# Row maxima of a quartered softmax: through memory instead of a masked product

## The chip, the cores and the metric

The kernel runs on one core of a Trainium2 chip. A core has a matrix engine (TensorE, PE in the profile), a vector engine (VectorE, DVE), an activation engine (ScalarE, ACT), a general engine (GpSimd, POOL) and an engine that only issues transfers (SyncE, SP). Each works through its own queue of instructions in order; semaphores tie the queues together. PE writes to PSUM[...]; all else lies in SBUF, on 128 partitions; DRAM is reached by DMA. The metric is the time of one execution on the device in microseconds.

## The reference, cut to what matters

The whole is one layer: a cross attention with residual, a block that sends a quarter of the tokens through self attention and the rest through a state-space scan, and a mixture of experts. The change lies in the cross attention:

```
sim = einsum("bihd,bjhd->bhij", q1, k) * scale   # 4 batches, 8 heads, 256 queries, 4096 + 256 keys
attn = softmax(sim, axis=-1)                     # subtracts each query's maximum over all keys
out = einsum("bhij,bjhd->bihd", attn, v)
```

All is in 32-bit floats. The softmax must hold for every query over its 4352 keys.

## The kernel before

The attention walks over 16 groups `G`, one for each batch and pair of heads, and in each over 8 blocks of 32 queries: 128 steps, numbered `n`, with `s` the number within the group. The keys of a group are cut into four quarters of 1088. In `scores(n)` (L1279, L1287) quarter `q` of the scores of the 32 queries goes to partitions 32q to 32q+31 of `su`, five PSUM banks that there are once only, so that a query has four partitions, one for each quarter, and both heads of the pair lie side by side. `su` is thus 128 partitions by 2 times 1088.

`copy_max(n)` (L1299) copies both halves out of `su` on DVE and keeps the maximum of each partition in `nm`, 128 by 2. These are maxima of quarters. To get a query's maximum, the kernel before does three things:

- on DVE it multiplies `nm`, repeated four times, by `quarter`, a mask that leaves the maxima of quarter q in columns of q alone: `mq`, 128 by 4 by 2 (L1306);
- in `stat(n)` PE multiplies `mq` by `same` (L1311), which has a 1 wherever two partitions belong to one query. Each partition then holds the four maxima of its query in eight columns (four quarters, two heads), in a free corner of `su`;
- DVE reduces them to `nb`, the negated maximum (L1316).

`exps(n)` (L1327, ACT) takes the exponential with `nb` as bias and sums it. `turn(n, j)` (L1336, DVE) transposes blocks of 32 by 32, and `values` (L1345, PE) multiplies four steps' worth by the values; this happens in steps with `s % 4 == 1`. `k_chunk` (L1226) and `v_chunk` (L1263) make keys and values of the same or the next group, three chunks in most other steps; ACT copies each from one of three PSUM banks (L1214, L1267). Their input `ctx` is loaded by SP through four buffers (L1130).

The order of instructions is written out by hand in one loop over `n`. One step issues: `scores(n)`, `exps(n-1)`, `copy_max(n)`, the first piece (a chunk, or nine key blocks of the values product), some background work, the second piece, then `turn(n-1, 0)`, `stat(n)`, `turn(n-1, 1)`, the third piece and background work again. In the steps with values `stat(n)` follows the second piece and both transposes come at the end. `slot(budget)` is what inserts background work: the router, the token attention, the scan and the expert ordering of the batches that are finished, whose generators yield a time until they are due and an amount of DVE time. The clock `now` that it compares with is advanced by hand-set estimates, 0.3 for `stat`. The scan (L632 to L652) runs on ACT (`da`), POOL (`db`, `y`) and DVE (L644) together.

After the attention, at about 1260 us, the scan of the last batch and the experts follow.

Of the kernel before, what the change touches and what calls it, by code (L numbers as in the profile page):

```python
# [8 lines left out]
F32 = mybir.dt.float32  # L9
AF = mybir.ActivationFunctionType  # L10
ALU = mybir.AluOpType
AX = mybir.AxisListType
PSUM = bass.MemoryType.PSUM

P = 128
# [22 lines left out]
def bc(ap, axis, n):  # L38

    ap = ap.unsqueeze(axis)  # L40
    shape = list(ap.shape)
    shape[axis] = n
    return ap.to_broadcast(shape)
# [3 lines left out]
def perceiver_layer(ctx: ExitStack, tc: tile.TileContext, a: dict, out: bass.AP):  # L47
    nc = tc.nc
# [5 lines left out]
    dram = ctx.enter_context(tc.tile_pool(name="dram", bufs=2, space=bass.MemoryType.DRAM))  # L54
    fin = ctx.enter_context(tc.tile_pool(name="fin", bufs=1))
# [999 lines left out]
    now = [0.0]  # L1055
    active = []

    def start(g):
        active.append([g, now[0], 0.0])
# [36 lines left out]
    SU = (0, 2 * 512 + 512 - (QK - SQ))  # L1096
    SC = (0, 3 * 512)
    SX = (2 * 512, SU[1])
    SM = 2 * 512 + 128
    NHP = H // 2  # L1100
    NG = B * NHP
    NJ = QK // 32
    with ExitStack() as s1:
        ctp = s1.enter_context(tc.tile_pool(name="xctx", bufs=4))
        wk = s1.enter_context(tc.tile_pool(name="xwk", bufs=2))
# [12 lines left out]
        def load_qk(G):  # L1118
            return load_weights(G, ("wk2",), "wk2", 2)

        def load_self(G):
            return load_weights(G, ("wk1", "wq1"), "wself", 1)
# [26 lines left out]
        def load_later():  # L1149
# [7 lines left out]
            yield from load_consts()  # L1157
            start(routed(0))

        same = fin.tile([P, 4, 32], F32, name="same")  # L1160
        dm = same[:, 0, :]
        nc.vector.tensor_reduce(
            out=dm, in_=ident.rearrange("p (c i) -> p i c", c=4), axis=AX.X, op=ALU.add
        )
        for q in range(1, 4):
            nc.vector.tensor_copy(same[:, q, :], dm)
        quarter = fin.tile([P, 4, 2], F32, name="quarter")
        nc.vector.tensor_reduce(
            out=quarter[:, :, 0], in_=ident.rearrange("p (c i) -> p c i", c=4), axis=AX.X,
            op=ALU.add,  # L1170
# [27 lines left out]
        su = ps_s.tile([P, 5 * 512], F32, name="su")  # L1198
# [7 lines left out]
        for t in qzs:  # L1206
            nc.gpsimd.memset(t, 0.0)
        kts, qTs, vts, sps, nbs, pts, pos, aos, lss = ({} for _ in range(9))
        mqs, nms = {}, {}

        def keys_out(G, k0, ps):

# [80 lines left out]
        def copy_max(n):  # L1293
            nms[n] = wk.tile([P, 2], F32, tag="nm", name="nm")
            sps[n] = [
                wk.tile([P, QK], F32, tag=f"sp{j}", name=f"sp{j}") for j in range(2)
            ]
            for j in range(2):
                nc.vector.tensor_scalar(  # L1299
                    out=sps[n][j], in0=su[:, SU[j] : SU[j] + QK], scalar1=1.0, scalar2=None,  # L1300
                    op0=ALU.mult, op1=ALU.max, accum_out=nms[n][:, j : j + 1],
                )


            mq = mqs[n] = wk.tile([P, 4, 2], F32, tag="mq", name="mq")
            nc.vector.tensor_tensor(mq, bc(nms[n], 1, 4), quarter, ALU.mult)  # L1306

        def stat(n):

            st = su[:, SM : SM + 8]  # L1310
            nc.tensor.matmul(  # L1311
                st, same.rearrange("p q i -> p (q i)"),
                mqs[n].rearrange("p q j -> p (q j)"), start=True, stop=True,
            )
            nbs[n] = wk.tile([P, 2], F32, tag="nb", name="nb")
            nc.vector.tensor_reduce(  # L1316
                out=nbs[n], in_=st.rearrange("p (q j) -> p j q", q=4), axis=AX.X, op=ALU.max,
                negate=True,
            )

        def exps(n):
            G, s = divmod(n, 8)
            b, hp = divmod(G, NHP)
            if n % 32 == 0:
                lss[b] = fin.tile([P, NHP, 8, 2], F32, tag="ls", name="ls", bufs=2)
            for j in range(2):
                nc.scalar.activation(  # L1327
                    sps[n][j], sps[n][j], AF.Exp, bias=nbs[n][:, j : j + 1],
                    accum_out=lss[b][:, hp, s, j : j + 1],
                )  # L1330
# [86 lines left out]
        with tc.manual_schedule():  # L1417
            norms = {}
            k_chunk(0, 0)
            wself[0] = load_self(0)  # L1420
            nc.scalar.dma_start(out=bo_bc, in_=a["xbo"].partition_broadcast(P))
            for _ in norm(0):
                pass
            for g in range(1, NCH):
                k_chunk(0, g)
                if g == 4:
                    turn_x(0)
            k_self(0)
            start(load_later())
            wv[0] = load_v(0)  # L1430
            N = 8 * NG
            for n in range(N + 2):
                G, s = divmod(n, 8)
                new, old = n < N, 1 <= n <= N


                pieces, took = [], 1.75
                if s == 5 and G + 1 < NG:
                    wv[G + 1] = load_v(G + 1)
                if s % 4 == 1:  # L1440
                    m, took = n // 4 - 1, 1.95
                    if m >= 0:
                        pieces = [
                            lambda i=i: values(m, i, min(i + 9, NJ)) for i in range(0, NJ, 9)
                        ]
                elif 2 <= s <= 4 and G < NG:
                    pieces = [
                        lambda g=g: v_chunk(G, g) for g in range(3 * s - 6, 3 * s - 3)
                    ]
                elif G + 1 < NG:  # L1450
                    if s == 0:
                        wqk[G + 1] = load_qk(G + 1)
                        wself[G + 1] = load_self(G + 1)
                    pieces = {
                        0: [lambda g=g: k_chunk(G + 1, g) for g in range(3)],
                        6: [lambda g=g: k_chunk(G + 1, g) for g in range(3, 6)],
                        7: [lambda: k_self(G + 1)]
                        + [lambda g=g: k_chunk(G + 1, g) for g in range(6, 8)],
                    }[s]


                tail = n >= N - 2

                def piece(i):
                    if i < len(pieces):
                        pieces[i]()
                    if i < len(pieces) or tail:
                        now[0] += took

                if new:  # L1470
                    scores(n)
                    now[0] += 2.1
                if old:
                    exps(n - 1)
                if new:
                    copy_max(n)
                piece(0)
                if s % 4 != 1:
                    slot(1.3)
                    piece(1)  # L1480
                    if old:
                        turn(n - 1, 0)
                    if new:
                        stat(n)
                        now[0] += 0.3
                    if s == 0 and n:
                        sums(G - 1)
                        now[0] += 0.2
                    if old:
                        turn(n - 1, 1)  # L1490
                    slot(1.3 if tail else 0.5)
                    piece(2)
                    slot(2.9)
                else:
                    last = s == 1 and G
                    if last:
                        spread(G - 1)
                        now[0] += 0.6
                    slot(1.5)
                    piece(1)  # L1500
                    if new:
                        stat(n)
                        now[0] += 0.3
                    slot(2.8)
                    if last:
                        normalize(m - 1)
                    if n == N + 1:

                        psx[B - 1] = bank("psx")
                        project(B - 1, 0, psx[B - 1], range(NHP))  # L1510
                        add(B - 1, 0, psx[B - 1])
                        project(B - 1, 1, psx[B - 1], range(NHP - 1))
                    piece(2)
                    slot(1.5)
                    piece(3)
                    if n > 4:
                        values_out(m)
                    if old:
                        turn(n - 1, 0)
                        turn(n - 1, 1)  # L1520
                    if last:
                        normalize(m)
                        if m % 8 == 7:
                            start_first(finish_batch(m // 8))
                b = n // 32 + 1
                if b < B:
                    if n % 32 == 20:
                        norms[b] = norm(b)
                    if n % 32 in (20, 22):
                        next(norms[b])  # L1530
                    if n % 32 == 29:
                        turn_x(b)
# [299 lines left out]
```

## Time and profile before

| what | value |
|---|---|
| median of three runs | 1555.44 us (1549.75 to 1558.04) |
| the profiled execution | 1555.58 us, of which the span of instructions is 1553.9 |
| PE, DVE, ACT, POOL busy in the span | 94%, 68%, 49%, 27% |
| mean granted PE clock | 0.977 of full speed |
| L1299, copy with maximum, DVE, 256 times | 1281 ns each |
| L1306, multiply to `mq`, DVE, 128 times | 167 ns median |
| L1311, the product, PE, 256 passes | 256 ns median |
| L1316, reduce to `nb`, DVE, 128 times | 128 ns median |
| L1327, exponential, ACT, 256 times | 1195 ns each |

A row of the group table or the timeline reads: line of the kernel, engine, operation, output and inputs by their names in the program, shapes, number of instructions, then busy time and mean, and in brackets how long the engine had been idle and what it had waited for. A 32-bit product is two passes on PE, so the trace counts 256 for 128 products. "PEld" is the loading of weights, which can lie beside matmuls. Matmuls are pipelined: their durations overlap, and what one costs is read from the distance of the pieces around it. The chain of work that ended last follows the program back from its last instruction, at each step to what released it; a piece in it is time on the path.

### The profile page before, as it was taken

The numbers are of one execution on the slowest core, as the hardware profiler recorded it, in microseconds if no ns is written. First come the engines' busy times: TensorE is split into PE (matmuls) and PEld (weight loads), VectorE is DVE, ScalarE is ACT, GpSimd is POOL, SyncE is SP. The second block draws the span as 40 slices with busy tenths as digits, with TensorE's granted clock in tenths as the row PEclk, the third lists the DMA queues.
The fourth block names the chain that finished last, engine by engine and source line by source line (L and its number), as shares of the span: only waits on it lengthen the run. The fifth ranks groups of instructions, "written<-read, shape, count | busy, mean of one in ns | idle before, by whom it ended". The sixth has DMA issues, their size and how long they took to land.

```text
span 1553.9 us, 37283 instructions
## 1 busy us (share of the span) xinstructions
PE 1461.9 (94%) x15686; PEld 1039.5 (67%) x15686; DVE 1057.1 (68%) x1812; ACT 758.9 (49%) x1486; POOL 412.0 (27%) x464
## 2 busy tenths in 40 slices
PE   7999999999999999999999999999998868988799
PEld 3757667576667475766665767757665558778587
DVE  1666666666699976565999866658988633499453
ACT  3444454454666644555667454546664413534211
POOL 1000000000089940000799500005996011110100
PEclk9999999999999999999999999999999968999899
DMA  7445543524344525243454343334543115777471
GB/s 240 149 131 160 161 139 107 180 72 143 120 147 140 182 83 192 79 145 100 141 176 158 113 144 126 99 112 162 159 127 114 42 55 183 253 250 259 125 233 48
DMA packets 157767, 223.41 MB, mean 144 GB/s; under 512 B 14976, under 2 KB 76160, under 8 KB 157600
## 3 DMA queue, kind: packets, MB, share of 16 engines
q1 hardware_dynamic: 152368, 211.45, 42.7%
q10 hardware_dynamic: 3744, 5.51, 1.1%
q0 software_dynamic: 1488, 4.07, 0.9%
q8 instruction: 124, 2.03, 0.5%
q14 instruction: 43, 0.35, 0.1%
HBM read 216.56 MB, written 4.42 MB: 142 GB/s over the span
## 4 chain that ended last, share of the span: by engine, by line
PE 63%; POOL 14%; DVE 13%; issue 4%; ACT 3%; DMA 2%; ACTq 0%; SPq 0%; DVEq 0%; POOLq 0%
PE po L1345 12%; PE su L1279 11%; PE psv L1263 11%; PE psk L1226 9%; POOL y L652 5%; POOL db L637 5%; POOL db L650 4%; DVE sp L1299 4%; PE su L1287 2%; PE pg L1749 2%; PE pu L1749 2%; PE pde L1762 2%; DVE pt L1336 2%; DVE db L739 1%; DVE db L644 1%
## 5 line engine op out<-in xcount | busy, mean ns | idle before, releaser
L1299 DVE TENSOR_SCALAR_CACHE_REDUCE sp<-su 128x1088 f32<-128x1088 f32 x256 | 318.8, 1281 | 182.0 <-PE su L1287 182.0
L1336 DVE STREAM_TRANSPOSE pt<-sp 128x1088 f32<-128x1088 f32 x256 | 328.0, 1295 | 57.0 <-PE po L1345 56.9
L1327 ACT ACTIVATE sp<-sp,nb 128x1088 f32<-128x1088 f32 x256 | 305.2, 1195 | 13.9 <-DVE nb L1316 13.7
L1345 PE MATMUL po<-pt,v 128*64 128x128 f32 x4352 | 263.9, 278 | 2.3 <-DVE pt L1336 1.3
L1279 PE MATMUL su<-kt,qz 64*32 64x512 f32 x4096 | 256.0, 609 | 4.4 <-DVE nb L1316 3.7
L1226 PE MATMUL psk<-ctx,wk 128*128 128x512 f32 x512 | 245.1, 612 | 10.2 <-DMA ctx<-in_ctxT 7.7
L1345 PEld LDWEIGHTS po<-pt,v 128*64 128x64 f32 x4352 | 241.7, 139 | 14.1 <-issue 7.7
L1263 PE MATMUL psv<-wv,ctx 128*128 128x128 f32 x2048 | 250.3, 279 | 0.6 <-DMA ctx<-in_ctxT 0.3
L1263 PEld LDWEIGHTS psv<-wv,ctx 128*128 128x128 f32 x2048 | 236.1, 192 | 6.7 <-issue 1.4
L1226 PEld LDWEIGHTS psk<-ctx,wk 128*128 128x128 f32 x512 | 91.4, 191 | 94.3 <-issue 85.0
L1214 ACT COPY kt<-psk 128x512 f32<-128x512 f32 x128 | 74.8, 585 | 158.6 <-PE psk L1226 158.4
L1279 PEld LDWEIGHTS su<-kt,qz 64*32 64x32 f32 x4096 | 63.3, 108 | 124.4 <-issue 93.0
L652 POOL TENSOR_TENSOR y<-y,db 128x192 f32<-128x192 f32 x192 | 135.2, 704 | 15.1
L1267 ACT COPY v<-psv 128x512 f32<-128x512 f32 x144 | 79.2, 558 | 119.8 <-PE psv L1263 118.5
L644 DVE TENSOR_TENSOR_SCAN db<-da,db 128x384 f32<-128x384 f32 x96 | 123.2, 1284 | 14.4 <-POOL db L637 3.7
L650 POOL TENSOR_TENSOR db<-db,cb 128x384 f32<-128x384 f32 x96 | 110.8, 1154 | 26.4 <-DVE da L642 26.4
L395 POOL TENSOR_TENSOR kbd<-qk,hmask 128x512 f32<-128x512 f32 x8 | 8.2, 1045 | 407.1 <-ACT qk L385 407.1
L637 POOL TENSOR_TENSOR db<-bb,xc 128x384 f32<-128x384 f32 x96 | 111.2, 1181 | 0.2
L1287 PEld LDWEIGHTS su<-kt,qz 128*32 128x32 f32 x2048 | 34.6, 109 | 109.3 <-issue 109.3
L632 ACT ACTIVATE da<-delta,A_log_sb 128x192 f32<-128x192 f32 x192 | 75.4, 447 | 51.1 <-DVE da L642 38.4
L1382 ACT COPY ao<-po 128x128 f32<-128x128 f32 x32 | 8.5, 264 | 152.5 <-PE po L1345 152.5
L1311 PEld LDWEIGHTS su<-mq,same 128*128 128x128 f32 x256 | 41.1, 191 | 54.7 <-DVE mq L1306 37.8
(278 smaller groups left out, 1587.2 us busy)
## 6 DMA issues: line engine op xcount, KB each, us to landing
ctx<-in_ctxT SPq DMA_DIRECT2D x256, 512.0 KB, 4.8
gateT<-in_gateT SPq DMA_DIRECT2D x27, 512.0 KB, 4.0
upT<-in_upT SPq DMA_DIRECT2D x27, 512.0 KB, 5.1
downT<-in_downT SPq DMA_DIRECT2D x27, 512.0 KB, 6.2
bb<-bcd SPq DMA_DIRECT2D x24, 192.0 KB, 4.3
cb<-bcd SPq DMA_DIRECT2D x24, 192.0 KB, 3.6
wv<-in_wv SPq DMA_DIRECT2D x32, 128.0 KB, 2.4
in_w<-in_in_w SPq DMA_DIRECT2D x32, 128.0 KB, 3.8
```

The lines of the kernel that those rows point to most:

```text
L637: nc.gpsimd.tensor_tensor(db, bbs[k], bc(xc[:, m, :], 1, SG), ALU.mult)
L644: nc.vector.tensor_tensor_scan(out=db, data0=da, data1=db, initial=0.0, op0=ALU.mult, op1=ALU.add,)
L650: nc.gpsimd.tensor_tensor(db, db, cbs[k], ALU.mult)
L652: nc.gpsimd.tensor_tensor(y[:, m, :], y[:, m, :], db[:, s, :], ALU.add)
L1226: nc.tensor.matmul(ps, wqk[G][:, 0, c, :], ct[:, c, :], start=(c == 0), stop=(c == KD - 1),)
L1263: nc.tensor.matmul(ps[:, i * P : (i + 1) * P], lhsT, wv[G][:, w, c, :], start=(c == 0), stop=(c == KD - 1),)
L1267: nc.scalar.copy(v.rearrange("p k d -> p (k d)"), ps[:, : n * P])
L1279: nc.tensor.matmul(su[q * 32 : (q + 1) * 32, SC[j] + lo : SC[j] + lo + 512], qT[r, j, s * 32 : (s + 1) * 32], kt[r, q, lo : lo + 512], sta ...
L1299: nc.vector.tensor_scalar(out=sps[n][j], in0=su[:, SU[j] : SU[j] + QK], scalar1=1.0, scalar2=None, op0=ALU.mult, op1=ALU.max, accum_out=nm ...
L1327: nc.scalar.activation(sps[n][j], sps[n][j], AF.Exp, bias=nbs[n][:, j : j + 1], accum_out=lss[b][:, hp, s, j : j + 1],)
L1336: nc.vector.transpose(pts[m, j][:, i, :], sps[n][j])
L1345: nc.tensor.matmul(pos[m][j * HD : (j + 1) * HD, :], vts[m // 2, k // 4][:, k % 4, j * HD : (j + 1) * HD], pts[m, j][:, :, kk * 32 : (kk + ...
```

## The change

The mask, the multiply and the product go. Instead, the maxima of the quarters are written to a small tensor in DRAM, `md`, in which a query's four quarters lie next to each other, and are read back with a source that repeats for the four groups of partitions. Each partition then has its query's eight values in SBUF, and the same reduce makes `nb` of them. Both transfers are issued from ACT's queue. `send_max(n)` comes after the first piece, `fetch_max(n)` where `stat(n)` was, and `stat(n-1)`, now only the reduce, comes in the next step between `scores(n)` and `exps(n-1)`. Of `same` only its first quarter, `dm`, is left, which other parts use.

```diff
-        same = fin.tile([P, 4, 32], F32, name="same")
-        dm = same[:, 0, :]
+        dm = fin.tile([P, 32], F32, name="dm")
...
-        for q in range(1, 4):
-            nc.vector.tensor_copy(same[:, q, :], dm)
...
-            mq = mqs[n] = wk.tile([P, 4, 2], F32, tag="mq", name="mq")
-            nc.vector.tensor_tensor(mq, bc(nms[n], 1, 4), quarter, ALU.mult)
+        def send_max(n):
+
+            mds[n] = dram.tile([32, 4, 2], F32, tag="md", name="md", bufs=4)
+            nc.scalar.dma_start(out=mds[n].rearrange("i q j -> q i j"), in_=nms[n])
+
+        def fetch_max(n):
+            mqs[n] = wk.tile([P, 4, 2], F32, tag="mq", name="mq")
+            nc.scalar.dma_start(
+                out=mqs[n].rearrange("p q j -> p (q j)"),
+                in_=mds[n].rearrange("i q j -> i (q j)").unsqueeze(0).to_broadcast([4, 32, 8]),
+            )
...
         def stat(n):
 
-            st = su[:, SM : SM + 8]
-            nc.tensor.matmul(
-                st, same.rearrange("p q i -> p (q i)"),
-                mqs[n].rearrange("p q j -> p (q j)"), start=True, stop=True,
-            )
             nbs[n] = wk.tile([P, 2], F32, tag="nb", name="nb")
             nc.vector.tensor_reduce(
-                out=nbs[n], in_=st.rearrange("p (q j) -> p j q", q=4), axis=AX.X, op=ALU.max,
+                out=nbs[n], in_=mqs[n].rearrange("p q j -> p j q"), axis=AX.X, op=ALU.max,
                 negate=True,
             )
...
                 if old:
+                    stat(n - 1)
                     exps(n - 1)
                 if new:
                     copy_max(n)
                 piece(0)
+                if new:
+                    send_max(n)
                 if s % 4 != 1:
                     slot(1.3)
                     piece(1)
+                    if new:
+                        fetch_max(n)
+                        now[0] += 0.3
                     if old:
                         turn(n - 1, 0)
-                    if new:
-                        stat(n)
-                        now[0] += 0.3
...
                     slot(1.5)
                     piece(1)
                     if new:
-                        stat(n)
+                        fetch_max(n)
                         now[0] += 0.3
```

More of the change, by code (lines that the diff above doesn't have):

```diff
@@ L1098, in perceiver_layer @@
     SX = (2 * 512, SU[1])
-    SM = 2 * 512 + 128
     NHP = H // 2
@@ L1208, in perceiver_layer @@
         kts, qTs, vts, sps, nbs, pts, pos, aos, lss = ({} for _ in range(9))
-        mqs, nms = {}, {}
+        mqs, nms, mds = {}, {}, {}
         def keys_out(G, k0, ps):
```

## The prediction

> **What bounds the kernel now.** I read the busy table first, then the waits, then the chain of work that ended last inside one group of steps, then one step's timeline.
>
> ```profile
> PE 1461.9 (94%) x15686; PEld 1039.5 (67%) x15686; DVE 1057.1 (68%) x1812; ACT 758.9 (49%) x1486; POOL 412.0 (27%) x464
> ...
> PE   7999999999999999999999999999998868988799
> ```
>
> TensorE (PE) is busy 94% of the span, 90% or more in all but the ends of the attention stage, which runs from about 25 to 1260 us in 128 steps. The other engines have room, so in that stage a microsecond counts if PE executes it or waits for it. The list of waits (total, times, longest), first of all engines, then of PE alone, says how much PE waits:
>
> ```profile
> DVE sp L1299 <- PE su L1287: 182.0, 69, 15.2
> ```
>
> ```profile
> PE su L1311 <- DVE mq L1306: 19.9, 14, 3.5
> ...
> PE su L1279 <- DVE nb L1316: 3.7, 3, 2.7
> ```
>
> VectorE (DVE) waits 182 us for PE's scores; PE waits only 19.9 us ahead of the maximum product (L1311) and 3.7 us ahead of scores for `nb`. The chain that ended last, in the stretch 137 to 176 us, gives the price of the product itself:
>
> ```profile
> 137.39 4.08 PE po L1345 x72
> 141.47 0.32 PE su L1311 x2
> 141.79 3.65 PE po L1345 x64
> ...
> 151.30 0.12 PE su L1311 x2
> 151.42 1.82 PE psk L1226 x4
> ```
>
> Columns are start, duration, work. The chain is PE without a gap, and the product sits in it: 0.12 us between key or value chunks, 0.32 us amid the values product. The group table's 0.24 us for each L1311 matmul overlaps its neighbours; the chain's piece is what the path pays.
>
> [...] the product's weights start to load at 48.34 us while `psv` matmuls run, so two 0.19 us loads cost only 0.12. [...]
>
> **The change part by part.** Product removed (L1311, 128 times): 97 steps at 0.12 us are 11.6 us, 31 steps that hold a values product at 0.32 us are 9.9 us; together 21.5 us of PE's path. Nothing covers it, so all of it is gain if PE stays the bound.
>
> Waits removed: 19.9, plus 2.6 for DVE `da` ahead of the same product in that list, plus 3.7, are 26.2 us. Most comes back: the next scores still overwrite `su`, so they wait for the copy of the same step. In 400 to 1150 us the product's waits are 5.9 + 2.6 = 8.5 us, caused by scans that make the copy late; PE then has other chunks to do, and I count half, 4 us. The other 17.7 us lie in the few steps at the start and end without enough chunks; there only the way from the copy to the read of `nb` goes, 40.06 to 40.92 us, 0.9 us in each of about five steps: 4 us. Together 8, between 3 and 17.
>
> VectorE: 128 multiplies `mq` (L1306, median 0.167 us, up to 0.82 beside POOL) go; the reduce to `nb` stays (0.13) and reads SBUF. That is 21 us or more off an engine that waits 182 us for PE: counted at zero, worth some microseconds in the scan stretches, where the chain does pass through it. Three setup copies vanish under the first 10 us of loads: zero.
>
> Two DMAs per step added on ACT, 256 in all, 1 KB out and 4 KB back (0.6 MB beside 223). An issue holds ACT's queue 0.33 us (the four `bcd` writes): 85 us over 128 steps, against ACT's 49% load, 60% in the scan stretches. What matters is the round trip:
>
> ```profile
> 44.91 1.29 DVE L1299 TENSOR_SCALAR_CACHE_REDUCE sp<-su 128x1088 f32<-128x1088 f32 x1 [1.63 <-PE su L1287]
> ...
> 47.34 0.08 DVE L1299 DVE_READ_ACCUMULATOR sp<-su 128x1 f32 x1
> ...
> 48.65 0.59 ACT L1267 COPY v<-psv 128x512 f32<-128x512 f32 x1 [1.20 <-PE psv L1263]
> ...
> 52.43 0.43 PE L1287 MATMUL su<-kt,qz 128*32 128x64 f32 x16
> ```
>
> ```profile
> bcd<-projT ACTq DMA_DIRECT2D x4, 24.0 KB, 1.4
> ...
> dt_w<-in_dt_w SPq DMA_DIRECT2D x3, 32.0 KB, 1.7
> ...
> routerT_sb<-in_routerT SPq DMA_DIRECT2D x1, 8.0 KB, 1.8
> ```
>
> The maxima are final at 47.42 us. The send is issued at 47.5; nearest write: `bcd`, 1.4 us; I take 1.4 to 2.1 (the 128 KB `ysd` writes), so it lands at 48.9 to 49.6. The fetch stands behind ACT's copy of the second chunk, over at 49.24, and behind the landing: issue at 49.3 to 49.7, with 1.7 to 2.1 for a small load it lands at 51.0 to 51.8. A round trip of 3.6 to 4.4 us. The reduce `nb` is now ahead of the next copy on DVE, and that copy needs scores that end at 52.86 - 0.12 = 52.74. So the fetch has about a microsecond to spare, and DVE would idle there anyway: zero on the path. Without that cover DVE's copy, the transposes and background scans behind it, and then the next scores are late by the excess.
>
> Exponentials, which start at 51.14 in the same timeline, move to about 51.2 to 52; behind them on ACT stand the chunk copies, whose three PSUM banks come round a chunk-cycle later: zero, up to 0.5 us per step where scans crowd ACT. ACT's send also waits for the copy, and the fetch for the send; behind them wait one chunk copy and the scans' decay factors. In the scan stretches ACT runs late already (exponentials near 4 us into the step), so I take 3 us in all, ends 0 and 28.
>
> SP: its loads share completion counters in turn with ACT's DMAs, so a context load can wait for a send some eight DMAs back. That has landed a step earlier, when the fourth context buffer comes free as well: zero; uncovered, part of a context load's 4.8 us. POOL's queue is not passed.
>
> Sum: 21.5 + 8 - 3 = 26.5 us. The profiled execution took 1555.58 us (span 1553.9 and 1.7 around it), 0.14 above the median of 1555.44. 1555.5 - 26.5 = 1529.
>
> **The rivals.** *Slower: the round trip becomes the loop.* From copy to copy there are now 2.5 us of copy, the trip and 0.13 of reduce. Eight steps last 68.3 us (`po` at 137.39 and 205.69), 8.54 each, less 0.17 for the product: 8.37. The trip decides from 8.37 - 2.63 = 5.7 us on, and each microsecond above costs 128 us. At 6.2 us: 1555.5 - 21.5 + 64 = 1598; at 7 us, 1700. For it: no row shows a store in 8-byte runs, context loads take 4.8 us to land on the same DMA engines, and 1 KB columns took 3.9 to 6.9 behind them. Against: those stood behind context loads on SP's own queue; `routerT`, 32-byte runs, took 1.8.
>
> *No change: ACT gives it back.* If the wait for the send and the later exponentials cost 0.5 us in each of some 55 steps with scans, that is 28 us: 1555. For it: the chain there passes DVE and POOL. Against: PE waits for ACT's chunk copies 0.6 us in 750.
>
> *Partial.* Only the product's time goes and waits return in full, with some late fetches: 10 us, 1545. *More.* All waits go and VectorE's relief counts: 1508. *The change does nothing*: excluded for the product, since the changed kernel issues none of the 128.
>
> **How the numbers follow.** A measurement of this kernel can tell about 0.5%, 7.8 us, from no change. Forecast, 1515 to 1541: 0.55. More: 0.07. Partial, to 1547: 0.09. No change: 0.09. Slower: 0.20, spread over 1564 to 1700. So faster 0.71, same 0.09, slower 0.20. A range of 1510 to 1575 leaves out most of the loop cases and a few below. The likeliest case alone: 1515 to 1541.
>
> **What would show it.** Right: no PE piece between chunks, short steps 7.9 instead of 8.02 us, values steps 0.3 shorter, the send landing in 1.4 to 2.1 us, DVE still waiting for `su` and not for `mq`. Wrong: DVE waits for the fetch for more than some 10 us, PE waits ahead of scores for DVE, or ACT's waits for the send push PE's chunks.

## The result, and the profile after

The changed kernel takes 1796.97 us (median of four runs, 1790.52 to 1803.1) against 1555.76 of the kernel before, also four runs: a ratio of 1.156, with a 95% interval of 1.153 to 1.158. It is slower by 241 us. The profiled execution took 1790.52 us, with a span of 1788.8. I read its views in the same order as before. First the busy table and the row of PE in 40 slices:

```profile
PE 1505.0 (84%) x15430; PEld 1032.2 (58%) x15430; DVE 1030.6 (58%) x1681; ACT 758.8 (42%) x1486; POOL 393.7 (22%) x464
...
PE   6878788888988979798898779888888786888799
```

The product's 256 passes are gone from the counts, as the prediction said. But PE fell from 94% to 84%, and no engine has taken its place: DVE is at 58%, ACT at 42%. When all engines have more room and the time is longer, I look for waits. (PE's busy time grew although it has less to do. Its mean granted clock fell from 0.977 to 0.924. In the kernels below the clock goes with PE's busy share: 0.976 to 0.980 at 94%, 0.951 to 0.966 at 89 to 90%, 0.907 at 81%; and e9, which keeps both transfers, has 0.980. So I take it as an effect of the idle time; no run tests that by itself, and what part of the loss the lower clock makes was not separated.)

The list of waits (total, times, longest), lines of DVE and ACT and then of PE:

```profile
DVE nb L1315 <- DMA mq<-md: 421.0, 107, 11.5
...
ACT kt L1210 <- DMA md<-nm: 101.9, 25, 7.4
...
ACT v L1263 <- DMA md<-nm: 89.7, 23, 7.5
...
DVE sp L1295 <- PE su L1283: 65.9, 30, 16.0
```

```profile
PE su L1275 <- DVE sp L1295: 60.9, 29, 7.2
PE su L1275 <- ACT kt L1210: 60.5, 13, 7.5
```

DVE's 182 us of waiting for scores became 66; in its place stand 421 us of waiting for the fetch, in 107 of 128 steps. On ACT, chunk copies stand 191.6 us behind sends, because the fetch ahead of them in the queue waits for the send to land. PE then waits 61 us for the copy of the scores and 61 for keys. The chain that ended last says it for the whole execution, by engine and by line:

```profile
DMA 39%; PE 28%; DVE 14%; ACT 10%; issue 6%; ACTq 1%; SPq 0%; POOL 0%; DVEq 0%; POOLq 0%
DMA md<-nm 23%; DMA mq<-md 14%; ACT sp L1326 6%; PE po L1344 5%; DVE sp L1295 5%; PE psk L1222 4%; PE su L1275 4%; DVE pt L1335 2%; PE psv L1259 2%; PE pg L1751 2%; PE pu L1751 1%; PE pde L1764 1%; DVE db L739 1%; DVE db L644 1%; PE su L1283 1%
```

Two DMAs of 1 and 4 KB are 37% of the path. In a stretch of plain steps the chain (start, duration, what) goes round without PE:

```profile
182.33 3.78 DMA mq<-md
...
186.13 0.17 DVE nb L1315
...
187.50 1.31 ACT sp L1326 x3
188.81 3.48 DMA md<-nm
...
192.31 2.97 DMA mq<-md
...
195.31 0.17 DVE nb L1315
...
197.96 8.37 DMA md<-nm
```

The timeline of the same step gives the loop's parts:

```profile
186.27 1.29 DVE L1295 TENSOR_SCALAR_CACHE_REDUCE sp<-su 128x1088 f32<-128x1088 f32 x1
...
188.69 0.08 DVE L1295 DVE_READ_ACCUMULATOR sp<-su 128x1 f32 x1
...
188.81 0.53 ACTq L1303 DMA_DIRECT2D md<-nm  x1
...
192.31 0.54 ACTq L1307 DMA_DIRECT2D mq<-md  x1
...
192.90 0.59 ACT L1210 COPY kt<-psk 128x512 f32<-128x512 f32 x1 [2.93 <-DMA md<-nm]
...
195.31 0.16 DVE L1315 TENSOR_REDUCE nb<-mq 128x2 f32<-128x8 f32 x1 [4.11 <-DMA mq<-md]
195.41 1.29 DVE L1295 TENSOR_SCALAR_CACHE_REDUCE sp<-su 128x1088 f32<-128x1088 f32 x1
```

From the end of the copy (188.77) to the reduce it takes 6.54 us: 3.5 for the send, 3.0 for the fetch, nothing else. From copy to copy it is 195.41 - 186.27 = 9.14 us, which is 2.50 of copies, the trip and 0.10 of the reduce. This stood in the prediction as the rival "the round trip becomes the loop". ACT has a second loop of the same length: the exponentials of step n-1 (2.4 us), which need the reduce, stand ahead of the send of step n in its queue, which is why the chain goes by `sp` L1326 rather than by the copies. The next send, at 197.96, took 8.37 us: six context and weight loads had been issued on SP's queue in the four microseconds before.

Taken over all 128 steps of the trace, the period, from one step's copy to the next, is 11.46 us against 9.57; 128 times the difference of 1.89 is 242 us, which is the whole loss.

### The profile page after: what moved, and what is told of

Same layout as the page of the kernel before. It is cut to its first block, busy times and chain, and to the rows that moved or that the text cites. A ratio compares the mean times of both kernels' runs of the same rounds, so it can differ in the third digit from the quotient of the medians.

```text
span 1788.8 us, 37224 instructions
## 1 busy us (share of the span) xinstructions
PE 1505.0 (84%) x15430; PEld 1032.2 (58%) x15430; DVE 1030.6 (58%) x1681; ACT 758.8 (42%) x1486; POOL 393.7 (22%) x464
## 4 chain that ended last, share of the span: by engine, by line
DMA 39%; PE 28%; DVE 14%; ACT 10%; issue 6%; ACTq 1%; SPq 0%; POOL 0%; DVEq 0%; POOLq 0%
DMA md<-nm 23%; DMA mq<-md 14%; ACT sp L1326 6%; PE po L1344 5%; DVE sp L1295 5%; PE psk L1222 4%; PE su L1275 4%; DVE pt L1335 2%; PE psv L1259 2%; PE pg L1751 2%; PE pu L1751 1%; PE pde L1764 1%; DVE db L739 1%; DVE db L644 1%; PE su L1283 1%
## 5 line engine op out<-in xcount | busy, mean ns | idle before, releaser
L1275 PE MATMUL su<-kt,qz 64*32 64x512 f32 x4096 | 294.0, 671 | 154.0 <-DVE sp L1295 60.9
L1326 ACT ACTIVATE sp<-sp,nb 128x1088 f32<-128x1088 f32 x256 | 305.5, 1194 | 223.5 <-DVE nb L1315 223.0
L1335 DVE STREAM_TRANSPOSE pt<-sp 128x1088 f32<-128x1088 f32 x256 | 321.4, 1288 | 43.7 <-PE po L1344 42.8
L1222 PE MATMUL psk<-ctx,wk 128*128 128x512 f32 x512 | 255.7, 642 | 11.3 <-DMA ctx<-in_ctxT 6.2
L1315 DVE TENSOR_REDUCE nb<-mq 128x2 f32<-128x8 f32 x128 | 20.2, 158 | 421.0 <-DMA mq<-md 421.0
L1344 PEld LDWEIGHTS po<-pt,v 128*64 128x64 f32 x4352 | 246.8, 141 | 13.2 <-issue 8.5
L1222 PEld LDWEIGHTS psk<-ctx,wk 128*128 128x128 f32 x512 | 100.0, 206 | 121.0 <-issue 104.8
L652 POOL TENSOR_TENSOR y<-y,db 128x192 f32<-128x192 f32 x192 | 141.0, 734 | 15.1
L650 POOL TENSOR_TENSOR db<-db,cb 128x384 f32<-128x384 f32 x96 | 99.9, 1041 | 119.3 <-DVE da L642 119.3
L637 POOL TENSOR_TENSOR db<-bb,xc 128x384 f32<-128x384 f32 x96 | 96.6, 1028 | 0.2
L1180 POOL TENSOR_TENSOR x_sb<-x_sb,xbo_bc 128x512 f32<-128x512 f32 x4 | 5.1, 1270 | 276.8 <-ACT x L211 266.2
```

The lines of the kernel that those rows point to most:

```text
L637: nc.gpsimd.tensor_tensor(db, bbs[k], bc(xc[:, m, :], 1, SG), ALU.mult)
L650: nc.gpsimd.tensor_tensor(db, db, cbs[k], ALU.mult)
L652: nc.gpsimd.tensor_tensor(y[:, m, :], y[:, m, :], db[:, s, :], ALU.add)
L1222: nc.tensor.matmul(ps, wqk[G][:, 0, c, :], ct[:, c, :], start=(c == 0), stop=(c == KD - 1),)
L1275: nc.tensor.matmul(su[q * 32 : (q + 1) * 32, SC[j] + lo : SC[j] + lo + 512], qT[r, j, s * 32 : (s + 1) * 32], kt[r, q, lo : lo + 512], sta ...
L1326: nc.scalar.activation(sps[n][j], sps[n][j], AF.Exp, bias=nbs[n][:, j : j + 1], accum_out=lss[b][:, hp, s, j : j + 1],)
```

## The experiments

There were two theories at the start. One: the trip is longer than the loop can hide (the reduce, with the next copy behind it, waits). The other: ACT's queue, held by the fetch that waits for the send, is what delays keys and values. Trip times below were worked out from the traces as means over 128 steps: "send" and "fetch" from issue to the last completion, "trip" from the end of the copy to the reduce, which includes DVE being busy elsewhere. "Plain" are the three groups from about 94 to 300 us, before there is background work; a figure for eight plain steps is the mean of the three. The "floor" is e1.

| kernel | us | ratio to before (95%) | period | send | trip |
|---|---|---|---|---|---|
| after | 1796.97 | 1.156 (1.153 to 1.158) | 11.46 | 4.6 | 8.4 |
| e1_floor | 1521.51 | 0.980 (0.976 to 0.983) | 9.33 | | |
| e2_stale | 1648.21 | 1.060 (1.058 to 1.063) | 10.33 | 5.1 | |
| e3_lines | 1645.67 | 1.059 (1.055 to 1.063) | 10.29 | 3.2 | 7.3 |
| e4_noctx | 1618.51 | 1.041 (1.039 to 1.044) | 10.11 | 3.8 | 7.2 |
| e5_order | 1730.17 | 1.114 (1.107 to 1.120) | 10.93 | 4.9 | |
| e6_order_lines | 1680.03 | 1.082 (1.077 to 1.088) | 10.60 | 3.2 | |
| e7_k16 | 1910.16 | 1.228 (1.221 to 1.235) | 12.46 | 3.9 | |
| e8_moved | 1554.56 | 1.001 (1.000 to 1.002) | 9.59 | | |
| e9_lines_noctx | 1517.08 | 0.976 (0.973 to 0.980) | 9.30 | 2.0 | 6.1 |
| e10_sums | 1656.28 | 1.065 (1.061 to 1.068) | 10.37 | | |
| e11_quadrants | 1606.81 | 1.033 (1.031 to 1.035) | 9.99 | | |
| e12_hybrid | 1538.59 | 0.991 (0.990 to 0.993) | 9.45 | | |

### What the product was worth, and which wait costs what

**e1_floor** is the kernel before without multiply, product and transfers:

```diff
-            mq = mqs[n] = wk.tile([P, 4, 2], F32, tag="mq", name="mq")
-            nc.vector.tensor_tensor(mq, bc(nms[n], 1, 4), quarter, ALU.mult)
...
-            nc.tensor.matmul(
-                st, same.rearrange("p q i -> p (q i)"),
...
-                out=nbs[n], in_=st.rearrange("p (q j) -> p j q", q=4), axis=AX.X, op=ALU.max,
+                out=nbs[n], in_=nms[n].unsqueeze(2), axis=AX.X, op=ALU.max,
```

> The kernel before with the multiply and the product taken out and nothing put in their place: each partition subtracts the maximum of its own quarter, so the softmax is not that of the reference. It prices the gain side of the prediction alone. If the 21.5 us of product and 8 us of waits were right, 1526 to 1532 us. If the product was hidden or its time comes back as waits, 1545 to 1556.

It took 1521.51 us beside 1553.9 for the kernel before, timed together: 32 us less. The gain that the change was to bring is there, and the sum is about the 29.5 us (21.5 + 8) that the prediction counted for it. The split of that sum is not confirmed. The same three chunks of keys in one plain step, in the chain of the kernel before (the product and the last chunk, 0.12 and 1.82 us, follow this piece) and in that of e1:

```profile
147.67 3.63 PE psk L1226 x8
```

```profile
143.01 5.35 PE psk L1226 x12
```

That is 3.63 + 0.12 + 1.82 = 5.57 against 5.35 us: the product costs 0.22, not 0.12, because the pieces around it are longer by 0.10 us as well. A step with values is shorter by 0.47 us in e1 (11.46 to 10.99), where the prediction counted 0.32. At these prices the product alone would be worth 97 x 0.22 + 31 x 0.47, about 36 us (an estimate from plain steps). So the product was priced too low, the 8 us of waits are not to be seen, and that the sum fits is in part luck. The loss of the changed kernel against this floor is 275 us.

**e2_stale** keeps both transfers, but the reduce reads the maxima fetched two steps earlier, so that DVE hardly ever waits for them:

```diff
-            mqs[n] = wk.tile([P, 4, 2], F32, tag="mq", name="mq")
+            mqs[n] = wk.tile([P, 4, 2], F32, tag="mq", name="mq", bufs=5)
...
-                out=nbs[n], in_=mqs[n].rearrange("p q j -> p j q"), axis=AX.X, op=ALU.max,
+                out=nbs[n], in_=mqs[n - 2 if n > 3 else n].rearrange("p q j -> p j q"), axis=AX.X, op=ALU.max,
```

> The changed kernel with both transfers in place, but the reduce reads the maxima fetched two steps earlier, so no instruction waits long for a transfer of its own step (any shift gives the same softmax, other maxima than the reference's are subtracted). Theory loop (copy, send, fetch, reduce, next copy follow one another, 2.5 + 8.4 us a step): the loop is cut, 1530 to 1570 us. Theory queue (ScalarE stands still for the send ahead of each fetch and that delays chunk copies and exponentials): the fetch still waits for the send, so most of the loss stays, over 1650 us.

It took 1648.21, between the two expectations and close to that of the queue: the cut of the loop brings 149 us, and 127 us above the floor remain. Its waits:

```profile
DVE sp L1295 <- PE su L1283: 229.7, 65, 15.5
...
ACT v L1263 <- DMA md<-nm: 127.3, 29, 8.2
...
ACT kt L1210 <- DMA md<-nm: 107.9, 28, 5.9
```

DVE waits for scores again, and ACT's chunk copies stand 235 us behind sends. Both limits are there. By these waits I put the remaining 127 us down to ACT's queue; the prediction had put 3, with 28 as its upper end. No run issues the transfers from another queue, which would have shown this share by itself.

### Why the trip is so long

In `md` of the changed kernel the stores of 8 bytes (one quarter of one query, both heads) lie without gaps, so that eight of them, the four quarters of two queries, share 64 bytes. **e3_lines** gives each store 64 bytes of its own, in four fixed tiles `mdp` of 32 by 4 by 16; the fetch then brings 256 bytes for each query in place of 32:

```diff
-            mds[n] = dram.tile([32, 4, 2], F32, tag="md", name="md", bufs=4)
-            nc.scalar.dma_start(out=mds[n].rearrange("i q j -> q i j"), in_=nms[n])
+            mds[n] = mdp[n % 4]
+            nc.scalar.dma_start(out=mds[n].rearrange("i q j -> q i j")[:, :, :2], in_=nms[n])
...
```

> The changed kernel with a DRAM layout in which every pair of maxima has 64 bytes of its own, so that the four DMA engines of a send no longer write into the same 32 bytes; the fetch brings 256 bytes a query instead of 32. Theory shared lines: the send's shortest time to landing falls from 3.4 to about 2.2 us, the trip's mean from 8.4 to about 7.2, the kernel to 1650 to 1690 us. Theory plain latency of small stores: send 3.4 as before, 1790 to 1810 us.

**e4_noctx** takes the other suspect away: the 512 KB context loads, of which only the first four are made, and their data used again:

```diff
+            if g % 4 in ctc:
+                return ctc[g % 4]
-            t = ctp.tile([P, KD, CK], F32, tag="ctx", name="ctx")
+            t = ctp.tile([P, KD, CK], F32, tag=f"ctx{g % 4}", name="ctx", bufs=1)
...
+            ctc[g % 4] = t
...
```

> The changed kernel with the context loaded only for the first four chunks and then reused, so keys and values are those of other tokens; some 250 loads of 512 KB are gone. Theory contention (the mean trip of 8.4 us is over its floor of 6.2 because the four DMA engines also carry context): the trip stays near 6.2 to 6.5 us in every step, the kernel at 1560 to 1610 us. If contention is not it, 1780 to 1800 us.

**e9_lines_noctx** has both edits together.

> e3 and e4 together: 64 bytes a pair, and no context loads after the first four (keys and values are those of other tokens). The trip should come down to about 4.5 us in every step, the value that the prediction took. If only the size of the trip was wrong in the prediction, 1525 to 1550 us; if its model of ScalarE's queue was wrong as well (the fetch's wait behind the send stops it even at this length), 1560 to 1600 us.

Either alone takes off more than half of the loss (151 and 178 us; e3 ends 4 us below what was expected, e4 8 above), both together take off all of it: 1517.08 us, at the floor and below the 1525 expected. The savings do not add; the account that fits is that the loop costs only what exceeds its cover. The kernel before was not run without its context loads. PE waits 8 us for context there, so I take the loads as such for a small part of this; that part was not measured. The shortest send separates the two: 3.3 us in after, 3.2 without context loads, 1.9 with 64 bytes for each store. So stores without gaps cost about 1.3 us even on quiet engines, and the loads add their part on top, 4.6 - 3.8, or 0.9 us of the mean before rounding. With both gone the send takes 2.0. The step of e9 in its timeline:

```profile
186.21 0.08 DVE L1304 DVE_READ_ACCUMULATOR sp<-su 128x1 f32 x1
...
186.32 0.53 ACTq L1312 DMA_DIRECT2D md<-nm  x1
...
188.31 0.54 ACTq L1316 DMA_DIRECT2D mq<-md  x1
...
190.69 0.17 DVE L1324 TENSOR_REDUCE nb<-mq 128x2 f32<-128x8 f32 x1 [1.99 <-DMA mq<-md]
...
191.57 1.29 DVE L1304 TENSOR_SCALAR_CACHE_REDUCE sp<-su 128x1088 f32<-128x1088 f32 x1 [0.71 <-PE su L1292]
```

The trip is 190.69 - 186.29 = 4.4 us, the upper end of what the prediction expected, and the next copy waits for scores (0.71), not for the fetch. This is the step that the prediction drew. (DVE still waits 92 us for fetches in e9, ahead of scores for which it would otherwise wait.)

All stores here are of 8 bytes, in both layouts; only those that lie without gaps are slow (3.3 us for the shortest send in after, 1.9 in e3), so the size of the store alone does not explain it.

**e7_k16** asked whether four DMA engines are too few. The send writes in the order of partitions, over 16 engines (the trace shows 16 completion writes for each send, 4 in after), and four fetches gather:

```diff
-            mds[n] = dram.tile([32, 4, 2], F32, tag="md", name="md", bufs=4)
-            nc.scalar.dma_start(out=mds[n].rearrange("i q j -> q i j"), in_=nms[n])
+            mds[n] = dram.tile([4, 32, 2], F32, tag="md", name="md", bufs=4)
+            nc.scalar.dma_start(out=mds[n].rearrange("q i j -> (q i) j"), in_=nms[n])
...
+            for g in range(4):
+                nc.scalar.dma_start(
+                    out=mqs[n][g * 32 : (g + 1) * 32], in_=mds[n].rearrange("q i j -> i q j"),
+                )
```

> The changed kernel with DRAM ordered by partition, so that a send is one run of 1 KB cut over 16 DMA engines instead of 4, each engine writing its own 64 bytes; the fetch has to be four DMAs of 8-byte runs, one for each group of partitions. Theory shared lines: the send lands in about 1.9 us at best, as in e3, and more engines bring nothing further. Theory engines (the send is slow because only four engines carry it): below 1.9. The three further issues of 0.54 us lengthen the trip by 1.6 us over e3: 1690 to 1800 us in both.

A miss: 1910.16. The four fetches of a step take 1.7 us (median; 2.0 in the mean) of ACT's queue in place of 0.54, and the send did not become fast. The send's line in the trace (minimum, median, maximum of its issue in ns, then of its landing in us):

```profile
L1303 ACTq DMA_DIRECT2D md<-nm x128: 338/344/419, 31.7 to 1613.1; - x128
...
DMA to landing us min/median/max: 2.7/3.5/5.6
```

The landing is still 2.7 us or more in this row, which covers only part of the sends (2.6 over all 128), so the theory of shared lines missed its 1.9, and that of the engines its "below 1.9". In the shortest send the 16 engines report one after the other, from 1.25 to 2.64 us. If each engine takes eight rows in order, which was expected and which no trace shows, it has 64 bytes to itself here; then 64 bytes shared between engines are not the cause. What the slow sends have in common is that their stores fill 1 KB without gaps; in e3 they lie 64 bytes apart over 8 KB. Which distance is enough was not tried. More engines were no remedy here.

### The order of the steps

Two things were moved beside the transfers: the reduce to the next step, ahead of exponentials and copy. **e8_moved** does only that in the kernel before, product kept:

```diff
                 if old:
+                    reduce(n - 1)
                     exps(n - 1)
```

> The kernel before with its product, only the reduce to nb moved into the next step ahead of the exponentials and the next copy, as in the changed kernel. Loop and queue theories: the move alone costs nothing, since product and reduce take 0.5 us and VectorE waits there for scores, 1550 to 1562 us. If the later exponentials are a cause of their own: over 1570 us.

1554.56 against 1554.46, ratio 1.0007 (0.9997 to 1.0017): the move is free. Its waits fit:

```profile
DVE nb L1318 <- PE su L1287: 177.3, 65, 6.8
```

The wait for scores, 182 us ahead of the copy before, now stands ahead of the reduce. It is the same wait.

**e5_order** is the changed kernel with the reduce and the exponentials behind copy, first piece and send, so that the trip has about 2.5 us more and the send no longer stands behind exponentials; **e6_order_lines** adds e3's `md`; **e10_sums** further puts `sums(G-1)` behind the third piece. The edits of e5 and of e10:

```diff
-                if old:
-                    stat(n - 1)
-                    exps(n - 1)
                 if new:
                     copy_max(n)
                 piece(0)
                 if new:
                     send_max(n)
+                if old:
+                    stat(n - 1)
+                    exps(n - 1)
```

```diff
-                    if s == 0 and n:
-                        sums(G - 1)
-                        now[0] += 0.2
                     if old:
                         turn(n - 1, 1)
                     slot(1.3 if tail else 0.5)
                     piece(2)
+                    if s == 0 and n:
+                        sums(G - 1)
+                        now[0] += 0.2
```

> The changed kernel with one thing moved: the reduce and the exponentials of step n-1 come after the copy of step n and after its send, so the copy no longer waits for the trip and the exponentials fill the time in which the fetch waits for the send. Transfers and layout as changed. Theory loop and queue together: both limits go, a trip of 8.4 us has about one step of 8.4 to hide in, 1535 to 1600 us. Theory that the transfers themselves are the load (issue time, DMA engines): 1700 or more.

> The same order as e5 and 64 bytes for each pair of maxima as in e3. A trip of about 7 us is then shorter than a step: 1522 to 1550 us, close to the 1521.5 of the floor and under the kernel before, if the length of the trip and its place in the order are the whole cause. If the fetch's wait still stops ScalarE: 1560 to 1620.

> e6 with the row sums of a group (a PE product that reads what the exponentials of the step add up) moved behind the third chunk of their step. In e6 the steps with s = 0 take 12.8 us in the plain stretch against 8.0 in the floor, the other chunk steps 7.3 to 8.4 as in the floor. If PE stands there for the late exponentials, those steps fall to 8 to 9 us and the kernel to 1620 to 1650 us. If context or the trip is the cause, 1670 to 1690 as e6.

Both were misses. e5 gained 67 us, but 1730.17 lies where the other theory, the transfers themselves as the load, had it; the waits name another cause. e6 was to take 1620 at most; at 1680.03 it is slower than e3, which has the same `md` and the order of the changed kernel. The exponentials now come late, and others wait for them. The waits of e6:

```profile
DVE pt L1340 <- ACT sp L1331: 162.5, 91, 2.9
...
PE psl L1363 <- ACT sp L1331: 30.8, 30, 4.6
```

The second of these is `sums(G-1)`, which stood ahead of PE's third piece in the first step of each group. e10 moved it: 30.8 became 9.6 us, and the first step of a plain group went from 12.78 to 9.07 us. The time fell by 24 us, to just above the interval expected. In eight plain steps e10 takes 69.0 us, before 68.8, e1 66.3, after 87.8; so what e10 still loses, 100 us against before, lies in the groups with background work. Which instruction there is late was not settled.

### A way without memory

**e11_quadrants** collects the four quarters with four small DVE copies across partitions and reduces four times, with no product and no transfer:

```diff
+            mq = wk.tile([32, 4, 2], F32, tag="mq", name="mq")
+            for q in range(4):
+                nc.vector.tensor_copy(mq[:, q, :], nms[n][q * 32 : (q + 1) * 32, :])
...
+            for q in range(4):
+                nc.vector.tensor_reduce(
+                    out=nbs[n][q * 32 : (q + 1) * 32, :], in_=mq.rearrange("p q j -> p j q"),
+                    axis=AX.X, op=ALU.max, negate=True,
+                )
```

> The kernel before without product and without memory: VectorE copies the maxima of the four groups of 32 partitions side by side (4 copies) and reduces them once into each group (4 reduces). About 8 times 0.06 to 0.15 us, 0.5 to 1.2 us of VectorE a step in place of 0.3. In plain steps VectorE has 2 us to spare, in the scan stretches little: 1525 to 1545 us if the spare time holds, 1550 to 1580 if the scan stretches pay for it.

Slower than either expectation, 1606.81, but in two parts: eight plain steps take 66.4 us, the floor's 66.3, and the loss is all in the scan stretches, where DVE is busy 96% (420 to 570 us). The same group of copies (count, then busy us and mean ns) in the windows 100 to 300 us and 420 to 570 us:

```profile
L1310 DVE COPY mq<-nm 32x2 f32<-32x2 f32 x96 | 14.3, 149 | 1.2
```

```profile
L1310 DVE COPY mq<-nm 32x2 f32<-32x2 f32 x56 | 22.4, 400 | 0.6
```

A copy that takes 149 ns alone takes 400 where POOL runs the scan's products (0.74 to 1.04 us each in that window; in the other one POOL does nothing of the scan). The four reduces keep their 151 ns in both. So the copies are long in the window where POOL is at work; why they are and the reduces are not was not shown. No run isolates it, nor the part that the added DVE work has in the loss even without it. **e12_hybrid** therefore uses the copies in the 55 steps without background scan and token attention, and the product in the other 73:

```diff
+        def busy(n):
+            return 34 <= n < 58 or 66 <= n < 91 or 98 <= n < 122
...
         def stat(n):
 
+            if not busy(n):
```

> The kernel before, with e11's copies and reduces on VectorE in the 55 steps without scan or token attention, and the product in the other 73. In the plain group of e11 eight steps took 66.4 us against 68.8 before, 0.3 us a step; 55 steps save 16 us: 1535 to 1543 us. If what e11 lost in the scan stretches comes from somewhere else than VectorE's load there, 1550 or more.

1538.59 us (five runs, 1537.6 to 1539.49) against 1552.04: ratio 0.991 (0.990 to 0.993). It is faster than the kernel before by 0.9%, which is little but more than either scatters, and within what was expected. Its copies stay short (minimum, median, maximum in ns):

```profile
L1317 DVE COPY mq<-nm x220: 112/156/160, 31.5 to 1234.4; 32x2 f32<-32x2 f32 x110
```

## Why the prediction was wrong, point by point

- **The bound was read rightly; the gain came out by luck in part.** PE was the bound, and taking the product away is worth 32 us (e1), where 21.5 + 8 were counted. But the product's piece in the chain, 0.12 or 0.32 us, is not all that the path pays: it is 0.22 and 0.47 in plain steps. That error and the 8 us of waits cancelled. That the moved reduce costs nothing is shown by e8.
- **The step that failed is the size of the trip.** The prediction took 1.4 to 2.1 us for the send, from `bcd`, and 3.6 to 4.4 for the trip, "about a microsecond to spare". In the changed kernel the send takes 3.3 at least and 4.6 in the mean, the fetch 3.2 in the mean, the trip 6.2 (lowest twentieth) to 8.4 (mean). `bcd` was the wrong row: it writes runs of 768 bytes, over 16 engines (16 completion writes). The prediction did say that no row shows a store in 8-byte runs, and bounded it by rows of another kind all the same.
- **The model behind it holds.** e9 brings the trip to 4.4 us in a quiet step and lands at the floor. The trip, once as short as predicted, is hidden as predicted. This is shown without context loads; with them no run has a trip as short.
- **The rival's formula was right where it was made, its slope was not general.** In the plain step shown the period is copy, trip and reduce, and the threshold of 5.7 us lies between a trip that is hidden (4.4, e9) and one that is not (6.5). But 128 us for each microsecond would make 1534 + 128 x (8.4 - 5.7), about 1880 us, of the mean trip; it is 1797. Steps with values or background work were longer from the start (11.45 and 10.63 us for the two with values in a plain group before) and so cover more: a plain group lost 18.9 us, a later one 14.1 in the mean (groups 4 to 14). The rival was given 0.20 and an upper end of 1700; the range ended at 1575.
- **"Context loads": named and then set aside.** The argument against, that late loads stood on SP's own queue, failed: the send at 197.96, on ACT's queue, took 8.37 us just after SP's loads. Without the loads the changed kernel is 178 us faster (e4). The other term on SP, loads that wait for sends and fetches, was put at zero. In the trace of before the DMAs of SP and ACT do share eight completion semaphores, in turn in 571 of 592 cases, and in after such waits came (48 us for 10 context loads), but PE's wait for context ahead of keys did not grow: 6.2 us, against 7.7 before.
- **The ACT term, "3 us, ends 0 and 28", was mis-sized.** It rested on a send that lands in 2 us. With the fetch waiting 3 to 4 us at the head of the queue, 127 us remain where DVE hardly waits for the data (e2). The reason given was the right one: the fetch waits for the send, and ACT's work behind it waits too (191.6 us of chunk copies behind sends in after). It was priced with the wrong duration.
- **An issue was put at 0.33 us**; the send's takes 0.525 and the fetch's 0.54. That is 0.4 us more in each step on a queue that is busy for 42% of the span; no run prices it by itself.
- **Of the signs listed**, the first came (no product between chunks, as also in the chain of e1); the landing in 1.4 to 2.1 and the short steps of 7.9 did not, and DVE waited for `su` 66 us where it had been 182; and all three named as wrong signs did: 421 us for the fetch, 61 ahead of scores, 192 of chunk copies behind sends.
- **Four engines carry a send or a fetch**, which no trace of the kernel before could show. In after each has four completion writes, behind an update about 0.96 us after its issue; a context load or a `bcd` write has 16. One write is read as one engine here.

## What to carry to other kernels

A value that goes to memory and back within a loop cost two whole DMA latencies here, one after the other: 4.4 us in the quiet step of e9, and 8.4 in the mean of the changed kernel, where large loads run beside it. Compare that with the slack of the loop at its worst, not at its mean, and price a small store by a row with the same run length and the same distance between stores, or leave the range open to the loop's formula. And a DMA that waits at the head of a computing engine's queue was a wait of that engine (191.6 us of ACT's chunk copies in after): price everything behind it.

## What the runs showed of the hardware that was not expected

- 128 stores of 8 bytes that lie without gaps in DRAM landed no earlier than 3.3 us after issue (3.2 in e2 and e4); with 64 bytes for each, 1.9 (e3). In a quiet send of after, at 44.77 us, the last packet starts 1.42 us after the issue, but the four engines report at 1.90, 2.77, 3.06 and 3.34 us, one after the other. In a quiet send of e3, at 43.60 us, the last packet of data starts at 1.42 us as well, and the four report between 1.86 and 1.93. So the added time lies behind the start of the packets. Why was not tried.
- 16 engines in place of four helped such a send little (2.6 at least, median 3.5), though its issue took 0.34 in place of 0.53 us.
- Small transfers on ACT's queue were held up by large loads from SP's: the send's mean falls from 4.6 to 3.8 us without the context loads, and single sends took over 8 us. How the DMA engines share themselves out was not tried.
- DVE copies of 32 by 2 elements took 149 ns alone and 400 in a stretch with POOL's scan work, while reduces of 32 by 8 elements took 151 ns in both (e11).
- A small product between two chunks on PE cost 0.22 us of the step, though its own piece in the chain is 0.12 (before and e1).
